# Attention values on half the rows: four full products and two 64-row pairs in place of three wide products

## The chip, the core and the metric

One NeuronCore of a Trainium2 chip runs the whole program. Its engines are TensorE (PE, with its weight loads shown as PEld), VectorE (DVE), ScalarE (ACT), GpSimd (POOL) and SyncE (SP), which here issues every DMA. The metric is the device time of one execution in microseconds, as the median of several runs.

## The reference

A macaron block on 4 sequences of 256 tokens with 512 features, all in fp32: half a feed-forward, attention, and the same half feed-forward again, each behind a layer norm and added to `x`.

```
x = x + 0.5 * ffn(layernorm(x))      # dense 512x512 + top-2 of 8 LoRA experts
x = x + attn(layernorm(x)) 
x = x + 0.5 * ffn(layernorm(x))

q, k, v = x @ wq, x @ wk, x @ wv     # 32 query heads, 8 key heads, 128 wide
q, k = rope(q), rope(k)
allowed = (j <= i) & (j > i - 128)   # a window of 128 keys
attn = softmax(where(allowed, q @ k.T / sqrt(128), min))
out = (attn @ v) @ wo
```

The change touches `attn @ v`.

## The kernel before

The work is cut into 2 halves of two sequences each, 8 key heads per half (`groups`, 16 pairs of half `h` and key head `g`), and 2 sequences per half: `units`, 32 triples (h, g, b). One unit handles 4 query heads (G) and the 256 queries of one sequence. Query, key, value and output projections use seven products of half size in place of eight (a Strassen-Winograd scheme), with sums of weights and tokens made on POOL and DVE.

**Scores** (`scores`, L730). The queries of a unit lie in 8 blocks of 32, with the four heads side by side, so that one matmul has 4 x 32 query rows. Blocks 0 to 3 (the first 128 queries) see keys up to their own block. Blocks 4 to 7 see the 128 keys of their window, and these are folded onto 128 places: the place of a key in the second half of the sequence is that of the key 128 earlier, whose turn in the window is over. `exponentials` (ACT), `normalize` (POOL) follow.

**Turning** (`turn_blocks`, L785, and `fetch`, L796). The probabilities have queries on the partitions; the value product needs keys there. DVE transposes 32x32 blocks in place (L791), one DMA for each half of the key blocks writes them to DRAM (`kept`, L792), and four DMAs, one for each of the four key blocks (L799), read them back into `turned`: partition = key place, then head, query block, query. The places that no query of a block sees are zeros set once at the start.

**Mask and values.** In the second 128 queries each place holds an old key for some queries and a new one for others. `split` (L804) writes `part`, the share of `turned` that belongs to new keys; on POOL (`affine_select`, L807) for b = 0 and for the last group, on DVE (a product with the constant `new`, L812) for b = 1. `difference` (L817) turns the second tile of values of each sequence into its difference to the first tile, and `values` (L822) then makes

```python
        for i, parts in enumerate((p0, p1)):
            po = (score_bank, mm_bank)[i](f"o{'ab'[i]}_{h}_{g}_{b}")
            for n, part in enumerate(parts):
                nc.tensor.matmul(
                    po, v[:, 2 * b + n, cols], part, start=(n == 0), stop=(n == len(parts) - 1)
                )
            nc.scalar.copy(oT[:, :, ts(i, P)], po.rearrange("p (j q) -> p j q", j=G))
```

that is, three products of 128 rows by 512 columns: `oa` = v0 with the first four query blocks, `ob` = v0 with the last four, plus (v1 - v0) with `part`. ACT copies both banks to `oT` (L832). `outputs` (L835) lets POOL make sums of `oT` and PE multiply with the output weights (`y`, L852).

**Order.** PE, DVE, ACT and POOL run in the order that the program writes; SP's DMAs are ordered by a scheduler that goes by their dependences. The loop over units looks one unit ahead. For b = 0, a string of letters sets the order: the digits are the products of the next group's queries (`queries`, `q` at L575, followed by the rotary sums on DVE, L523 and L525, and POOL, `qT` at L531), `T` and `U` turn the probabilities of the current unit, `t` is the mask, `S` the next unit's scores, `y` an output product of the unit before. For b = 1, the next key or value projection (`k` at L632, `v` at L684) stands between. In both, `values` is followed by the first products of the next keys, values or queries, and then by the first `y` product.

**Homes.** `turned` and `probs` exist once; `part` is a pool tile with one buffer. The layer norm's scaled tiles `xc` have three buffers of their own; `hl` and `ht` (router and expert columns) have homes sized for four tiles.

Of the kernel before, what the change touches and what calls it, by code (L numbers as in the profile page):

```python
# [38 lines left out]
def macaron_kernel(  # L39
# [154 lines left out]

    def by_heads(dst, make):
        make(dst, 0)
        other = sb.tile(list(dst.shape), F32, tag="by_heads", bufs=1, name=f"{dst.name}_hi")
        for j in range(1, G):
            make(other, j * BLK)
            nc.gpsimd.tensor_copy(dst[ts(j, BLK), :], other[ts(j, BLK), :])  # L200
# [32 lines left out]
    turned = const.tile([P, G, 2 * NB, BLK], F32, name="turned")  # L233
    for e in range(NB - 1):
        nc.gpsimd.memset(probs[:, e + 1 :, e, :], 0.0)
    for c in range(1, NB):
        nc.gpsimd.memset(turned[ts(c, BLK), :, :c, :], 0.0)


    old = const.tile([P, NB, BLK], F32, name="old")  # L240
    nc.gpsimd.memset(old, 1.0)
    nc.gpsimd.affine_select(
        out=old, in_=old, compare_op=ALU.is_gt,
        fill=0.0, base=0, pattern=[[-BLK, NB], [-1, BLK]], channel_multiplier=1,
    )
    new = const.tile([P, NB, BLK], F32, name="new")
    nc.gpsimd.tensor_scalar(new, old, -1.0, 1.0, ALU.mult, ALU.add)

    rank = const.tile([P, E], F32, name="rank")
    for e in range(E):  # L250
# [18 lines left out]
    def scale(t, tag):  # L269
        if (tag, t) not in moments:  # L270
            measure(t, tag)
        mv, std = moments[tag, t]
        std = std or deviation(t, tag, mv)
        rstd = sb.tile([P, 1], F32, tag="rstd", bufs=4, name=f"rs_{tag}_{t}")
        nc.vector.reciprocal(rstd, std)
        xc = sb.tile([P, D], F32, tag="xc", bufs=3, name=f"xc_{tag}_{t}")
        if tag == "f1":
            shift = sb.tile([P, 1], F32, tag="shift", bufs=4, name=f"sh_{tag}_{t}")
            nc.vector.scalar_tensor_tensor(shift, mv[:, 0:1], -1.0, rstd, ALU.mult, ALU.mult)
            cols = slice(D // 2 if t < 2 else 0, D)  # L280
            if t < 2:
                lo = slice(0, D // 2)
                nc.vector.tensor_scalar(xc[:, lo], xt[t][:, lo], mv[:, 0:1], rstd, ALU.subtract, ALU.mult)
            nc.scalar.activation(xc[:, cols], xt[t][:, cols], AF.Identity, bias=shift, scale=rstd)
        else:
            nc.vector.tensor_scalar(xc, xt[t], mv[:, 0:1], rstd, ALU.subtract, ALU.mult)
        if far(t, tag):
            nc.vector.transpose(xc, xc)
            away = dram.tile([KC, P, P], F32, tag="away", name=f"away_{tag}_{t}")
            nc.sync.dma_start(  # L290
                out=away.rearrange("c p x -> p c x"), in_=xc.rearrange("p (c x) -> p c x", c=KC)
            )
            xc = away
        moments[tag, t] = xc

    def far(t, tag):
        return tag == ("a" if t >= TPH else "f2")
# [56 lines left out]
    def ffn(tiles, tag, then):  # L354
# [22 lines left out]
        def narrow(i):  # L377
            t = tiles[i]
            if i == 0:
                state["hl"] = sb.tile([P, TPH, E * R + E], F32, tag="hl", name=f"hl_{tag}_{t0}")[:, :n, :]  # L380
            pa = score_bank(f"pa_{tag}_{t}")
            for c in range(KC):
                nc.tensor.matmul(  # L383
                    pa[:, : E * R + E], x_of(i, c), ar_sb[:, c, :],
                    start=(c == 0), stop=(c == KC - 1),
                )
            nc.scalar.copy(state["hl"][:, i, :], pa[:, : E * R + E])
# [84 lines left out]
        def gated():  # L472
            hl = state["hl"]
            pt = ps.tile([P, n, P], F32, tag="s", bufs=4, name=f"ph_{tag}_{t0}")
            for i in range(n):
                nc.tensor.transpose(pt[:, i, :], hl[:, i, : E * R], ident)
            state["ht"] = sb.tile([P, TPH, P], F32, tag="ht", bufs=1, name=f"ht_{tag}_{t0}")
            nc.scalar.copy(state["ht"][:, :n, :], pt)

        def leave(i):  # L480
            bank, t = po.pop(i), tiles[i]
# [184 lines left out]
    def project_values(h, g):  # L666
# [36 lines left out]
        def others():  # L703
            product(2, c11)
            product(4, c21)
            add(v21, c21, u2)
            product(3, c12)
            nc.scalar.copy(v11, c11)
            add(v12, c12, u2)
            difference(h, g)  # L710

        return first, both, second, others

# [71 lines left out]
    def turn_blocks(pr, name, c):  # L785

        if c == 0:
            kept[name] = dram.tile([P, NB, 2 * NB * BLK], F32, tag="kept", name=f"kept_{name}")
        if True:
            w = pr[:, c : c + 2].rearrange("p c n k -> p (c n k)")  # L790
            nc.vector.transpose(w, w)  # L791
            nc.sync.dma_start(  # L792
                out=kept[name][:, c : c + 2, :], in_=pr[:, c : c + 2].rearrange("p c n k -> p c (n k)")
            )

    def fetch(name):  # L796
        heads = kept.pop(name).rearrange("(j k) c x -> k j c x", j=G)
        for c in range(NB):
            nc.sync.dma_start(  # L799
                out=turned[ts(c, BLK), :, c:, :].rearrange("p j n q -> p j (n q)"),  # L800
                in_=heads[:, :, c, c * BLK :],
            )

    def split(h, g, b):  # L804
        part = sb.tile([P, G, NB, BLK], F32, tag="part", bufs=1, name=f"part_{h}_{g}_{b}")
        if b == 0 or (h, g) == groups[-1]:
            nc.gpsimd.affine_select(  # L807
                out=part, in_=turned[:, :, NB:, :], compare_op=ALU.is_ge, fill=0.0, base=0,
                pattern=[[0, G], [BLK, NB], [1, BLK]], channel_multiplier=-1,
            )  # L810
        else:
            nc.vector.tensor_tensor(  # L812
                part, turned[:, :, NB:, :], new.unsqueeze(1).to_broadcast([P, G, NB, BLK]), ALU.mult
            )
        return [turned[:, :, :NB, :]], [turned[:, :, NB:, :], part]

    def difference(h, g, tiles=slice(None)):  # L817

        pairs = vS[h, g].rearrange("p (b i) f -> p b i f", i=2)[:, tiles]
        nc.vector.tensor_tensor(pairs[:, :, 1], pairs[:, :, 1], pairs[:, :, 0], ALU.subtract)  # L820

    def values(h, g, b, p0, p1):  # L822
        oT = sb.tile([HD, G, S], F32, tag="oT", bufs=4, name=f"oT_{h}_{g}_{b}")
        v = vS[h, g - g % 2]
        cols = ts(g % 2, HD)
        for i, parts in enumerate((p0, p1)):
            po = (score_bank, mm_bank)[i](f"o{'ab'[i]}_{h}_{g}_{b}")
            for n, part in enumerate(parts):
                nc.tensor.matmul(  # L829
                    po, v[:, 2 * b + n, cols], part, start=(n == 0), stop=(n == len(parts) - 1)  # L830
                )
            nc.scalar.copy(oT[:, :, ts(i, P)], po.rearrange("p (j q) -> p j q", j=G))  # L832
        return oT

    def outputs(h, g, b, oT):  # L835
# [162 lines left out]
    def run(queue, n):  # L998
        for _ in range(min(n, len(queue))):
            queue.popleft()()  # L1000
# [24 lines left out]
    for u, (h, g, b) in enumerate(units):  # L1025
# [11 lines left out]
        def turn_half(c):  # L1037
            once(f"t{c}{ahead[-1]}", lambda: turn_blocks(ahead[0], ahead[-1], c))
# [9 lines left out]
        fill(left, 0)  # L1048
        if left == 1:
            nc.scalar.activation(root, eps, AF.Sqrt)  # L1050
        parts = []

        def look_ahead(at=u + 1):
            nonlocal ahead
# [4 lines left out]
            add_sums(h - 1, BPH - 1, nc.gpsimd, slice(-2, None))  # L1059
            sum_weights("v", *groups[n])  # L1060

        def part(at=(h, g, b)):
            parts.extend(split(*at))

        if b == 0 and n < len(groups):

            order = {0: "1n6kTvD2U75tS4r3n", 4: "1Eyn6TaW2U7cyXx5dtSy4re3yVn"}[len(late)]
            steps = queries(*groups[n], nc.scalar.copy, ends)  # L1070
            steps |= {
                "y": lambda: run(late, 1), "r": invert, "n": level, "S": look_ahead,
                "E": lambda: exponentials(*ahead, which=range(NB, 2 * NB)),
                "D": lambda: difference(0, 0, slice(1)),
                "W": lambda: sum_o_weights(h, g, ("t3", "t1")), "X": lambda: sum_o_weights(h, g, ("t2",)),
                "x": between_halves if (h, g) == groups[NKV + 1] else None,
                "V": lambda: sum_o_weights(h, g, ("t4",)), "v": lambda: project_v(0, 0, 2),
                "k": lambda: sum_weights("k", *groups[2]), "a": lambda: fill(left, 1),
                "T": lambda: turn_half(0), "U": turn, "t": part, "c": None, "d": None, "e": None,
            }  # L1080

            if g == NKV - 2 and h + 1 < NHALF:
                more_tokens = sum_tokens(h + 1, *(nc.gpsimd, nc.vector) * 2)
                steps |= {"c": more_tokens[3], "d": more_tokens[1], "e": more_tokens[2]}
            for step in order:
                if steps[step]:
# [2 lines left out]
        elif b == 1 and n + 1 < len(groups):  # L1089
# [24 lines left out]
            elif n % 2 == 0 and n + 2 < len(groups):  # L1114
                load_v(*groups[n + 2])
            run(late, len(late) - 1)
            for t in shifted:
                norm_attn(t, scaled=True)
        else:
# [15 lines left out]
            load_q(*groups[n + 1])  # L1135
        if b == 0 and 1 < n < len(groups):
            load_o(*groups[n])
        if not parts:
            part()
        fill(left, 2)  # L1140
        run(late, len(late) - 1)
        early = ahead[-1] == "{}_{}_{}".format(*units[u + 1]) if left > 1 else False
# [7 lines left out]
        if u == 0:  # L1150
            project_v(0, 0, 3)
            load_v(*groups[2])
        oT = values(h, g, b, *parts)
        if u == 0:
            difference(0, 0, slice(1, 2))
        if b == 0 and n + 1 < len(groups):

# [79 lines left out]
```

## Time and profile before

| | |
|---|---|
| Median of 3 runs | 740.49 us (740.28 to 740.81) |
| Profiled execution | 740.92 us, its span 739.2 us |
| PE busy | 728.7 us (99%) |
| DVE, POOL, ACT busy | 562.5, 562.1, 195.1 us |
| Granted TensorE clock | 1.0 (mean of the execution) |
| DMA | 82.87 MB on the program's queue, 35.4% of 16 engines' span |

The span runs from the first to the last instruction that the profile shows; the execution is 1.72 us longer. Busy time counts records, and matmul records overlap, since each is shown until its result is written. Idle time of an engine that is not the last to finish costs nothing.

### The profile page before, as it was taken

Reading aid. Unit: us, or ns where it says so; the run is one execution under the profiler, and the core shown is the slowest. Engines: PE = TensorE matmul, PEld = TensorE weight load, DVE = VectorE, ACT = ScalarE, POOL = GpSimd, SP = SyncE. Lnnn points to the kernel's source line nnn. Section 1 sums busy time; section 2 is a strip of 40 time slices with the busy share of each in tenths; the row PEclk is TensorE's granted clock in tenths of the full one; section 3 lists DMA queues with packets and bytes.
Section 4 is the critical chain, followed back from the end, with each engine's and each line's share of the span. In section 5 each row is a group of like instructions: output and inputs, shape, how many; then the busy total and the mean of one; then the engine's idle time right before and its main releaser. Section 6 shows DMA issues by size and latency. Waiting matters only on the chain.

```text
span 739.2 us, 11048 instructions
## 1 busy us (share of the span) xinstructions
PE 728.7 (99%) x3606; PEld 603.3 (82%) x3606; DVE 562.5 (76%) x1297; ACT 195.1 (26%) x724; POOL 562.1 (76%) x613
## 2 busy tenths in 40 slices
PE   8999999999999999998999999999999999999998
PEld 6878888888888888886888888888888888888766
DVE  5797895878786878778677867586877867795877
ACT  5520223332222212130222233222123031222331
POOL 6878878777968686859878699868686878976753
PEclk9999999999999999999999999999999999999999
DMA  9301251424245433625142424242332415433201
GB/s 315 141 1 37 89 177 44 155 65 152 92 155 137 149 98 107 186 69 187 53 167 70 137 83 152 81 166 80 118 129 68 150 53 177 116 124 84 71 29 58
DMA packets 78249, 83.58 MB, mean 113 GB/s; under 512 B 21232, under 2 KB 50928, under 8 KB 78192
## 3 DMA queue, kind: packets, MB, share of 16 engines
q1 hardware_dynamic: 78192, 82.87, 35.4%
q8 instruction: 29, 0.48, 0.3%
q14 instruction: 28, 0.23, 0.1%
HBM read 61.88 MB, written 20.97 MB: 112 GB/s over the span
## 4 chain that ended last, share of the span: by engine, by line
PE 84%; POOL 6%; DVE 5%; issue 3%; DMA 1%; SPq 0%; ACT 0%; DVEq 0%; POOLq 0%
PE q L575 24%; PE y L852 22%; PE ob L829 7%; PE v L684 6%; PE k L632 6%; PE sb L753 4%; PE sa L739 3%; PE oa L829 3%; PE p_f L419 3%; PE po_f L419 2%; PE po_f L482 1%; PE y L894 1%; POOL x L393 1%; PE pa_f L383 1%; PE pv L720 1%
## 5 line engine op out<-in xcount | busy, mean ns | idle before, releaser
L531 POOL TENSOR_TENSOR qT<-ra_q,rb_q 128x512 f32<-128x512 f32 x64 | 81.8, 1279 | 74.8 <-DVE rb_q L525 74.8
L525 DVE TENSOR_TENSOR rb_q<-q,sin_sb 64x512 f32<-64x512 f32 x128 | 88.1, 688 | 1.7
L772 ACT ACTIVATE probs<-probs,mx 128x32 f32<-128x32 f32 (+3 forms) x128 | 44.7, 351 | 144.8 <-DVE mx L742 144.8
L779 POOL TENSOR_TENSOR probs<-probs,sm 128x512 f32<-128x512 f32 x64 | 65.7, 1046 | 6.1 <-DVE sm L1031 6.1
L869 DVE TENSOR_TENSOR x<-y,x 128x256 f32<-128x256 f32 (+1 forms) x62 | 34.2, 551 | 41.5 <-PE y L852 41.3
L852 PE MATMUL y<-wot,oT 128*128 128x256 f32 x248 | 63.7, 379 | 0.4 <-DVE rb_q L525 0.4
L852 PE MATMUL y<-wo,oT 128*128 128x256 f32 x248 | 63.7, 379 | 0.0
L832 ACT COPY oT<-oa 128x512 f32<-128x512 f32 x32 | 18.7, 585 | 169.1 <-PE oa L829 169.1
L852 PE MATMUL y<-wo,oTs 128*128 128x256 f32 x244 | 62.6, 379 | 0.0
L575 PE MATMUL q<-xs,wq 128*128 128x256 f32 x256 | 60.6, 379 | 0.2 <-DVE rb_k L525 0.2
L575 PE MATMUL q<-xs,wqs 128*128 128x256 f32 x256 | 60.6, 380 | 0.0
L575 PE MATMUL q<-xa,wq 128*128 128x256 f32 x256 | 60.5, 379 | 0.0
L575 PEld LDWEIGHTS q<-xa,wq 128*128 128x128 f32 x256 | 48.5, 190 | 12.5 <-issue 4.1
L575 PEld LDWEIGHTS q<-xs,wqs 128*128 128x128 f32 x256 | 48.5, 190 | 7.3 <-PE y L852 0.4
L575 PEld LDWEIGHTS q<-xs,wq 128*128 128x128 f32 x256 | 48.5, 190 | 7.0 <-issue 0.5
L791 DVE STREAM_TRANSPOSE probs<-probs 128x512 f32<-128x512 f32 x64 | 43.7, 700 | 10.8 <-POOL probs L779 10.4
L852 PEld LDWEIGHTS y<-wo,oTs 128*128 128x128 f32 x244 | 46.4, 190 | 6.3
L852 PEld LDWEIGHTS y<-wot,oT 128*128 128x128 f32 x248 | 45.8, 190 | 6.5 <-POOL wot L171 0.8
L852 PEld LDWEIGHTS y<-wo,oT 128*128 128x128 f32 x248 | 45.9, 190 | 5.3
L523 DVE TENSOR_TENSOR ra_q<-q,cos_sb 128x512 f32<-128x512 f32 x64 | 43.9, 686 | 6.3 <-PE q L575 2.0
L772 ACT ACTIVATE probs<-sb,mx 128x128 f32<-128x128 f32 x128 | 44.6, 357 | 0.0
L126 POOL TENSOR_TENSOR oTs<-oT 128x256 f32<-128x256 f32 x31 | 22.9, 740 | 23.5 <-ACT oT L832 23.5
(220 smaller groups left out, 1726.7 us busy)
## 6 DMA issues: line engine op xcount, KB each, us to landing
wq<-in_wq_dram SPq DMA_DIRECT2D x16, 1024.0 KB, 5.6
wo<-in_wo_dram SPq DMA_DIRECT2D x16, 1024.0 KB, 5.2
kept<-probs SPq DMA_DIRECT2D x64, 256.0 KB, 2.2
wk<-in_wk_dram SPq DMA_DIRECT2D x8, 512.0 KB, 4.3
wv<-in_wv_dram SPq DMA_DIRECT2D x8, 512.0 KB, 4.1
turned<-kept SPq DMA_DIRECT2D x32, 128.0 KB, 2.6
turned<-kept SPq DMA_DIRECT2D x32, 112.0 KB, 2.9
turned<-kept SPq DMA_DIRECT2D x32, 96.0 KB, 2.6
```

What stands on the lines that cost most here:

```text
L419: nc.tensor.matmul(bank[:, ts(i, D // 2)], lhs[j][m - 1][:, c, :], weights["bs"][m - 1][:, c, :], start=(m in (1, 5, 2, 4) and c == 0), st ...
L523: nc.vector.tensor_tensor(twice(a), twice(src), angle(cos_sb), ALU.mult)
L525: nc.vector.tensor_tensor(twice(b[o : o + half, :]), twice(src[i : i + half, :]), angle(sin_sb[o : o + half, :]), ALU.mult,)
L531: nc.gpsimd.tensor_tensor(dst, view(a), view(b), ALU.add)
L575: nc.tensor.matmul(bank[:, ts(j, S)], w[:, c, ts(j, HD)], x[:, c], start=(new and j == 0 and c == 0), stop=(c == 1), skip_group_check=True,)
L632: nc.tensor.matmul(dst, w[n - 1][:, c, :], x[n - 1][:, c], start=(start and c == 0), stop=(c == 1), skip_group_check=True,)
L684: nc.tensor.matmul(bank[:, i, :], x[n - 1][:, c, i, :], w[n - 1][:, c, :], start=(start and i == 0 and c == 0), stop=(c == 1), skip_group_ ...
L772: nc.scalar.activation(dst, src, AF.Exp, bias=mx[:, n : n + 1], scale=scale, accum_out=sm[:, n : n + 1])
L779: nc.gpsimd.tensor_tensor(w, w, sm.unsqueeze(1).unsqueeze(3).to_broadcast([P, 2, 2 * NB, BLK]), ALU.mult)
L791: nc.vector.transpose(w, w)
L829: nc.tensor.matmul(po, v[:, 2 * b + n, cols], part, start=(n == 0), stop=(n == len(parts) - 1))
L852: nc.tensor.matmul(py[:, ts(i, D // 2)], lhs[n - 1][:, c, :], weights["os", h, g][n - 1][:, c, :], start=(i == 0 and c == 0), stop=(c == 1 ...
```

## The change

`values` now makes eight products. Query blocks 2 and 3 use v0 over all 128 places (128 columns each). Blocks 6 and 7 use `w`, which holds v1 in its lower 64 rows and v0 in its upper 64; blocks 4 and 5 use v0 (256 columns each). Block 0 needs only places 0 to 63, and block 1 too: block 0 runs over the lower 64 rows, and block 1 over the upper 64, for which its keys (`aside`) and values (`vD`) are kept a second time there. In blocks 4 and 5 only the lower places hold new keys beside old ones, in 6 and 7 only the upper: `part` now holds these halves, and its two products have 64 rows each. `mixture` copies the values into `vW` and `vD` on ACT; `difference` comes later in the program. The blocks are written to DRAM by four DMAs and read back by one for `turned`, one for `aside` and two for `part`, which `split` masks in place. ACT copies the two banks out in four pieces.

With it go new homes for `xc` (`ra`, `rb`, `u2`), `hl` and `ht`; three of four token sums at the half's end go to POOL, and in the order string of these units `e` comes before `S`.

```diff
-    for c in range(1, NB):
-        nc.gpsimd.memset(turned[ts(c, BLK), :, :c, :], 0.0)
...
+    part = const.tile([P, G, NB // 2, BLK], F32, name="part")
+    aside = const.tile([P, G, BLK], F32, name="aside")
...
-        xc = sb.tile([P, D], F32, tag="xc", bufs=3, name=f"xc_{tag}_{t}")
+        home, bufs = (("xc", "u2"), 1) if far(t, tag) else (("ra", "rb"), 2)
+        xc = sb.tile([P, D], F32, tag=home[t % 2], bufs=bufs, name=f"xc_{tag}_{t}")
...
-            difference(h, g)
+            mixture(h, g)
...
-            kept[name] = dram.tile([P, NB, 2 * NB * BLK], F32, tag="kept", name=f"kept_{name}")
-        if True:
-            w = pr[:, c : c + 2].rearrange("p c n k -> p (c n k)")
-            nc.vector.transpose(w, w)
-            nc.sync.dma_start(
-                out=kept[name][:, c : c + 2, :], in_=pr[:, c : c + 2].rearrange("p c n k -> p c (n k)")
-            )
+            kept[name] = dram.tile([G, NB, BLK, 2 * NB * BLK], F32, tag="kept", name=f"kept_{name}")
+        w = pr[:, c : c + 2].rearrange("p c n k -> p (c n k)")
+        nc.vector.transpose(w, w)
+        for i in (c, c + 1):
+            nc.sync.dma_start(out=kept[name][:, i], in_=pr[:, i].rearrange("p n k -> p (n k)"))
...
+        heads = kept.pop(name).rearrange("j c k x -> (c k) j x")
+        nc.sync.dma_start(out=turned.rearrange("p j n q -> p j (n q)"), in_=heads)
+        nc.sync.dma_start(out=aside[high], in_=heads[low, :, BLK : 2 * BLK])
+        for rows, n in ((low, NB), (high, NB + 2)):
+            nc.sync.dma_start(
+                out=part[rows].rearrange("p j n q -> p j (n q)"),
+                in_=heads[rows, :, n * BLK : (n + 2) * BLK],
+            )
...
+        engine = nc.gpsimd if b == 0 or (h, g) == groups[-1] else nc.vector
+        engine.tensor_tensor(part, part, new.unsqueeze(1).to_broadcast([P, G, NB // 2, BLK]), ALU.mult)
...
+        for i, rows in ((1, low), (0, high)):
+            nc.scalar.copy(vW[h, g][rows, tiles], pairs[rows, :, i])
+        nc.scalar.copy(vD[h, g][high, tiles], pairs[low, :, 0])
...
+        add(pb[:, n : 2 * n], v0, turned[:, :, 3, :], start=True, stop=True)
+        add(pa[:, n : 2 * n], v0, turned[:, :, 2, :], start=True, stop=True)
+        add(pb[:, 2 * n :], w, turned[:, :, 6:8, :])
+        add(pa[:, 2 * n :], v0, turned[:, :, 4:6, :])
+        add(pa[:, :n], v0[low], turned[low, :, 0, :], stop=True)
+        add(pb[:, :n], v0_low, aside[high], stop=True)
+        add(pa[:, 2 * n :], dv[low], part[low], stop=True)
+        add(pb[:, 2 * n :], dv[high], part[high], stop=True)
+        blocks_of = oT.rearrange("p j (n q) -> p n j q", q=BLK)
+        for i, po in enumerate((pa, pb)):
+            nc.scalar.copy(blocks_of[:, i:NB:2], po[:, : 2 * n].rearrange("p (n j q) -> p n j q", n=2, j=G))
+        for i, po in enumerate((pa, pb)):
+            nc.scalar.copy(
+                oT[:, :, P + i * S // 4 :][:, :, : S // 4], po[:, 2 * n :].rearrange("p (j q) -> p j q", j=G)
+            )
...
-            order = {0: "1n6kTvD2U75tS4r3n", 4: "1Eyn6TaW2U7cyXx5dtSy4re3yVn"}[len(late)]
+            order = {0: "1n6kTvD2U75tS4r3n", 4: "1Eyn6TaW2U7cyXx5dteSy4r3yVn"}[len(late)]
...
-                more_tokens = sum_tokens(h + 1, *(nc.gpsimd, nc.vector) * 2)
+                more_tokens = sum_tokens(h + 1, *(nc.gpsimd,) * 3, nc.vector)
...
+            if n % 2 == 0:
+                difference(*groups[n])
```

In it `n` is 128 (G x BLK), `low` and `high` are rows 0 to 63 and 64 to 127, `pa` and `pb` are two PSUM banks.

## The prediction

> **What bounds the kernel now.** I read the page's busy times first, then its chain of waits, then the matmul groups with shapes kept apart, then the chain in order of time, then the timeline of one unit.
>
> ```profile
> span 739.2 us, 11048 instructions
> PE 728.7 (99%) x3606; PEld 603.3 (82%) x3606; DVE 562.5 (76%) x1297; ACT 195.1 (26%) x724; POOL 562.1 (76%) x613
> ...
> PE 84%; POOL 6%; DVE 5%; issue 3%; DMA 1%; SPq 0%; ACT 0%; DVEq 0%; POOLq 0%
> ```
>
> TensorE is idle for 739.2 - 728.7 = 10.5 us of the span, and the chain that ended last is 84% PE. So time taken from PE's stream comes off the end nearly one for one, and time taken from DVE, ACT or POOL comes off nowhere. The profiled execution took 740.92 us, 1.72 over its span and 0.43 over the median of 740.49; I sum against 740.92 and take the 0.43 off at the end.
>
> The groups of matmuls (mean is a record's duration; a program's fp32 matmul is two records, two weight loads):
>
> ```profile
> L829 PE MATMUL ob<-part,v 128*128 128x512 f32 x64 | 33.0, 597 | 1.3 <-POOL part L807 1.0 <-DVE part L812 0.3
> ...
> L829 PE MATMUL oa<-turned,v 128*128 128x512 f32 x64 | 32.8, 593 | 0.5 <-issue 0.5
> L829 PE MATMUL ob<-turned,v 128*128 128x512 f32 x64 | 32.7, 592 | 0.0
> ...
> L684 PE MATMUL v<-wv,xs 128*128 128x128 f32 x112 | 14.8, 275 | 0.0
> ```
>
> Every group is 128*128: no matmul of before works on 64 rows, which is what the change adds. Durations overlap; the price is the spacing, from the chain in order of time (start, length):
>
> ```profile
> 216.51 1.72 PE ob L829 x4
> 218.23 1.78 PE v L684 x16
> 220.88 4.46 PE v L684 x40
> 225.35 3.46 PE y L852 x16
> ```
>
> Four 512-column records take 1.72, so a 512-column matmul costs 0.86 us. Sixteen 128-column records take 1.78: 0.223 per matmul. Sixteen 256-column records take 3.46: 0.432 per matmul. The three products of a unit are 3 x 0.86 = 2.59 us; 32 units make 82.8 us.
>
> The timeline of one b = 1 unit, for what the values wait for:
>
> ```profile
> 263.19 0.94 SPq L792 DMA_DIRECT2D kept<-probs  x2
> ...
> 265.28 2.08 SPq L799 DMA_DIRECT2D turned<-kept  x4
> ...
> 267.96 1.05 PE L739 MATMUL sa<-kT,qT 128*128 128x32 f32 x8
> ...
> 268.86 1.25 PE L753 MATMUL sb<-kT,qT 128*128 128x160 f32 x8
> ...
> 270.54 1.65 DVE L812 TENSOR_TENSOR part<-turned,new 128x512 f32<-128x512 f32 x1 [0.15 <-DMA turned<-kept]
> ...
> 271.67 1.02 PE L829 MATMUL oa<-turned,v 128*128 128x512 f32 x2
> ```
>
> The mask starts 0.15 us after the last load, PE 1.1 us after that: the transfers are close behind the end.
>
> **The products, full part.** Four full products replace part of the work: two of 128 columns and two of 256, 2 x 0.223 + 2 x 0.432 = 1.31 us.
>
> **The products, pairs.** Four matmuls over 64 rows remain: 128 low (`turned`), 128 high (`aside`), 256 low and 256 high (`part`), in this order. One after another they cost the same 1.31 us; the unit is then 2.62, 0.03 more than now, +1.1 us over 32 units. If each pair ran wholly side by side, 0.655 is saved: 1.965, -0.62 a unit, -19.9 us. These are the two ends for the overlap. I take neither. The records of one matmul sit on the same rows, so they follow each other, and PE takes records in order; then only neighbours on different halves overlap: second record of the low 128 with the first high (0.111), the next two (0.111), and second low 256 with first high 256 (0.216). That is 0.438 saved, if weights can be loaded into both halves at once. If loads follow each other, the floor shows in `sa`: eight records of 32 to 128 columns take 268.86 - 267.96 = 0.90, 0.112 each, though narrow ones need less. Loads in line then leave only about 0.23 saved. I take 0.438, since the loads belong to different rows: 2.62 - 0.438 = 2.18, -0.40 a unit.
>
> **The change of shape.** Each unit goes once from 128 rows to 64 and once back. No row shows that. Bounds: nothing (a gain is excluded, there is nothing to overlap that is not counted above), and at most a record's tail plus an uncovered weight load. The tail is duration less spacing, 0.379 - 0.216 = 0.163; the load before a matmul is 0.21 (its load row starts at 254.82 in the same view, its matmul at 255.03). So 0 to 0.37 a switch, two a unit: 0 to 23.9 us. I take half a tail, 0.08, nearer to the low end since loads of before run ahead of their matmuls everywhere: +0.16 a unit.
>
> The Trainium skill (TensorEngine Tiling (Array Packing), Key Properties) says that a change of the tiling mode drains the TensorE, which speaks against this change; it gives no time, and no run here shows it. With the whole tail of 0.163 a switch, my sum would gain 0.08 a unit instead of 0.24, 2.5 us in all.
>
> So PE gains 0.40 - 0.16 = 0.24 us a unit, 7.7 us.
>
> **Transfers.** SP issues eight a unit in place of six: four `kept` writes, one `turned`, one `aside`, two `part`. Two `kept` issues take 0.94 now; four go out by about 264.4, and the last lands 2.2 later (the page's median for `kept`), 266.6. The single `turned` load needs all four; it is 512 KB of 128x4x256, the shape of the `wk` and `wv` loads, which land in 4.3 and 4.1: 270.8. The `part` loads, issued 0.4 apart behind it on the same queue, land near 271.2; the mask (128x256; 606 ns in the row of `v` at L820, where the wider one has a median of 822) ends near 271.8. PE first needs `turned` at 271.67 and `part` some 1.6 later: margins of 0.9 and 1.4. Behind the mask DVE has the next scores' maxima, held some 0.6 us; ACT alone reads them next, and it sits idle 144.8 us for them already. In b = 0 units the mask is POOL's and today ends 5.5 us ahead of its product (290.53 against 296.07 in the next unit); behind it wait the `qT` sums, for which POOL idles 74.8 us. The price is 0 if the margins hold, and if each of 14 b = 1 units lost 0.5 us, 7 us. I take 0.5 in all.
>
> The skill (DMA: Bandwidth & Descriptors, Specifications) wants pieces of at least 512 B for line rate; the `part` and `aside` pieces are 256 and 128 B. The `xa` loads of before have 128 B pieces and land in 2.4 us, like others of their size, so here the row speaks for no extra cost.
>
> **Other engines.** `oT` comes out in four copies of 256 columns (372 ns, the L641 row) in place of two of 585. The last three follow the last matmul, so `oT` is whole some 1.1 us after it, not 0.6; the first reader, the y product, has its weights loaded 1.35 after (259.12 against 257.77). Cover gone, each unit would lose the difference. `mixture` adds three ACT copies of 64x512 a pair of groups, some 14 us in all on an engine 26% busy, hidden by its waits for `mx`. `difference` goes later on DVE, behind these copies; POOL's mask keeps its 0.73 us, DVE's halves: off the path. The renamed homes of `xc`, `hl` and `ht`, the startup tables, and one token sum that goes from DVE to POOL: nothing, hidden under PE's stream; uncovered, 1.3 us for the sum, once.
>
> **Sum.** 740.92 - 7.7 + 0.5 - 0.43 = 733.3 us.
>
> **Rivals.** *Nothing runs side by side.* Then 64 rows cost as much as 128, +1.1 us plus 0.5 for transfers: 742.1. For it: no row shows overlap. Against it: each member of a pair has its own rows and its own bank (`pa`, `pb`). The change then doesn't do what it says. *The switch eats the gain.* This one ends slower. It sits at the first 64-row matmul and at the first full one after it. It decides from 0.20 us a switch (half of 0.40); at 0.37 it costs 0.74 - 0.40 = +0.34 a unit, +10.9: about 751.9. With loads in line, 0.10 a switch is enough. For it: the tail and the load are real in the rows; against it: loads run ahead now. *The load comes late.* The overlap pays its 7.7, but `turned` misses its margin by 0.5 in the b = 1 units: +7, 739.8; no difference that counts. *No switch cost, weights in parallel*: -12.9 + 0.5, 728.1.
>
> **How the numbers follow.** 0.2%, about what a measurement of this kernel tells from no change, is 1.5 us. The overlap paying (728 to 739): 0.59, in it 0.15 for the free switch. No difference, mostly the late load or a switch near 0.20: 0.11. Slower: 0.30, of which no overlap 0.12 and the switch 0.18. Faster and slower both hold weight, so the likeliest case's own range is 728 to 739; eight in ten needs the other sides: 727 to 747, which leaves out the dearest switch and whole pairs side by side.
>
> **What would show it.** Right: in the groups, 64-row matmuls at L838; in the timeline, the eight products of a unit from first start to the next matmul in 2.3 to 2.4 us, the high 128 starting before the low one's second record ends; PE still 99% busy. A gap of 0.2 or more ahead of the first 64-row record or behind the last is the switch. A unit of 2.62 is no overlap. If PE waits at its first product for `turned`, the transfers decide. I am wrong if PE's idle time grows by more than 5 us.

## The result, and the profile after

The changed kernel takes 875.0 us (872.4 to 876.7, 4 runs) against 740.4 for the kernel before on the same chip: a ratio of 1.181, with an interval of 1.178 to 1.185. It is 134.6 us slower, far outside the range. The profiled execution took 876.0 us. Lines from its page (here and below, rows that the argument does not need are left out):

```profile
span 874.3 us, 11949 instructions
PE 767.3 (88%) x3926; PEld 641.6 (73%) x3926; DVE 553.3 (63%) x1296; ACT 215.0 (25%) x815; POOL 556.4 (64%) x612
PEclk9999889999898999899998999898999999999899
PE 45%; DMA 31%; DVE 12%; POOL 6%; issue 3%; SPq 3%; ACT 0%; DVEq 0%; POOLq 0%; ACTq 0%
```

TensorE was idle for 10.5 us of the span before; now it is idle for 874.3 - 767.3 = 107.0. Its busy time grew too, 728.7 to 767.3, although it has less to multiply. And DMA, 1% of the chain that ended last, is now 31%. The row of slices gives a reason for the second: the granted clock dips all along the execution (mean 0.941, before 1.0).

The waits (engine and what it waited for: us in total, times, longest):

```profile
POOL part L810 <- DMA part<-kept: 96.6, 16, 12.4
PE ob L838 <- DMA turned<-kept: 93.9, 26, 7.1
DVE part L810 <- DMA part<-kept: 92.1, 15, 7.3
```

PE waits at the first value product of 26 of the 32 units, for the load of `turned`. The timeline of one b = 1 unit, to set beside the one of before (SPq rows are issues: start, time that SP took, how many):

```profile
301.56 2.33 SPq L796 DMA_DIRECT2D kept<-probs  x4
304.00 0.60 SPq L100 DMA_DIRECT2D wk<-in_wk_dram  x1
306.90 0.63 SPq L801 DMA_DIRECT2D aside<-kept  x1
310.63 0.37 SPq L800 DMA_DIRECT2D turned<-kept  x1
314.90 0.77 PE L838 MATMUL ob<-turned,v 128*128 128x128 f32 x2 [4.69 <-DMA turned<-kept]
315.26 0.43 DVE L810 TENSOR_TENSOR part<-part,new 128x256 f32<-128x256 f32 x1 [6.50 <-DMA part<-kept]
```

The four writes are issued by 303.89. The load of `turned` needs all of them and goes out at 310.63, 6.7 us later. Before, the second write was issued by 264.13; the first load, which reads only the first write's blocks, went out 1.15 us after that (265.28), and the third load, the first to read the second write's, 2.45 us after it (266.58). PE now waits 4.69 us, and then the unit's products need 3.95 us from first start to the next matmul. Over these 3.95 us (314.90 to 318.85) the mean granted clock is 0.57.

A unit that does not wait looks like this (start, from first to last end):

```profile
680.42 0.38 PE L838 MATMUL ob<-turned,v 128*128 128x128 f32 x2
680.64 0.39 PE L838 MATMUL oa<-turned,v 128*128 128x128 f32 x2
680.86 0.60 PE L838 MATMUL ob<-turned,vw 128*128 128x256 f32 x2
681.29 0.90 PE L838 MATMUL oa<-turned,v 128*128 128x256 f32 x3
681.82 0.18 PEld L838 LDWEIGHTS oa<-turned,v 64*128 64x128 f32 x1 [0.33 <-issue]
682.14 0.38 PE L838 MATMUL oa<-part,v 64*128 64x256 f32 x1
682.15 0.38 PE L838 MATMUL ob<-part,v 64*128 64x256 f32 x1
682.67 1.13 PE L636 MATMUL k<-xa,wk 128*128 128x256 f32 x4
```

682.67 - 680.42 = 2.25 us (2.26 with the trace's third decimal). In the kernel before, the unit that starts at 271.67 ends with this row's start:

```profile
274.25 1.89 PE L575 MATMUL q<-xa,wq 128*128 128x256 f32 x8
```

274.25 - 271.67 = 2.58. After, the low and high products over `part` start together. The products do what the change says. It is their operands that come too late.

### The profile page after: what moved, and what is told of

The parts are those of the page before. It is cut to its first block, busy times and chain, and to the rows that moved or that the text cites. A ratio compares the mean times of both kernels' runs of the same rounds, so it can differ in the third digit from the quotient of the medians.

```text
span 874.3 us, 11949 instructions
## 1 busy us (share of the span) xinstructions
PE 767.3 (88%) x3926; PEld 641.6 (73%) x3926; DVE 553.3 (63%) x1296; ACT 215.0 (25%) x815; POOL 556.4 (64%) x612
## 4 chain that ended last, share of the span: by engine, by line
PE 45%; DMA 31%; DVE 12%; POOL 6%; issue 3%; SPq 3%; ACT 0%; DVEq 0%; POOLq 0%; ACTq 0%
DMA kept<-probs 20%; PE q L579 15%; DMA turned<-kept 10%; PE oa L838 7%; PE y L874 7%; PE ob L838 4%; PE v L688 4%; PE k L636 3%; DVE rb_q L529 2%; SPq L796 2%; DVE q L558 2%; DVE probs L794 1%; DVE ra_q L527 1%; POOL oTs L126 1%; PE p_f L423 1%
## 5 line engine op out<-in xcount | busy, mean ns | idle before, releaser
L838 PE MATMUL ob<-turned,v 128*128 128x128 f32 x64 | 18.9, 388 | 94.0 <-DMA turned<-kept 93.9
L838 PEld LDWEIGHTS ob<-turned,v 128*128 128x128 f32 x64 | 12.8, 244 | 104.5 <-issue 104.3
L850 ACT COPY oT<-oa 128x256 f32<-128x256 f32 x32 | 11.9, 372 | 311.5 <-PE ob L838 311.5
L810 POOL TENSOR_TENSOR part<-part,new 128x256 f32<-128x256 f32 x17 | 12.3, 726 | 96.6 <-DMA part<-kept 96.6
L579 PE MATMUL q<-xa,wq 128*128 128x256 f32 x256 | 65.3, 399 | 0.0
L810 DVE TENSOR_TENSOR part<-part,new 128x256 f32<-128x256 f32 x15 | 6.4, 425 | 92.1 <-DMA part<-kept 92.1
L838 PE MATMUL oa<-turned,v 128*128 128x128 f32 (+2 forms) x192 | 62.6, 431 | 0.0
L838 PEld LDWEIGHTS oa<-turned,v 128*128 128x128 f32 (+1 forms) x192 | 43.7, 261 | 20.4 <-issue 16.7
```

Source lines behind the costliest of these rows:

```text
L579: nc.tensor.matmul(bank[:, ts(j, S)], w[:, c, ts(j, HD)], x[:, c], start=(new and j == 0 and c == 0), stop=(c == 1), skip_group_check=True,)
L810: engine.tensor_tensor(part, part, new.unsqueeze(1).to_broadcast([P, G, NB // 2, BLK]), ALU.mult)
L838: nc.tensor.matmul(dst, v, p, start=start, stop=stop, skip_group_check=True)
```

## The experiments

The questions were: is the loss the products or the transfers; if transfers, which part; and what do the products give when nothing waits. All medians stand beside 740.4 to 741.3 for the kernel before on the same chip. "Idle" is span less PE busy time; busy time, idle time and clock are those of the profiled execution.

| kernel | us | ratio | PE busy | idle | clock |
|---|---|---|---|---|---|
| before | 740.4 | | 728.7 | 10.5 | 1.0 |
| after | 875.0 | 1.181 | 767.3 | 107.0 | 0.941 |
| before, after's writes | 827.1 (one run) | | 759.6 | 65.8 | 0.964 |
| after, writes by head | 868.1 | 1.172 [1.170, 1.173] | 766.6 | 99.8 | 0.945 |
| the same, other order of pairs | 869.9 | 1.173 [1.171, 1.176] | 766.4 | 97.7 | 0.944 |
| after, four loads | 850.2 (one run) | | 764.0 | 84.5 | 0.950 |
| after, writes by head and half | 817.0 | 1.103 [1.100, 1.106] | 748.9 | 71.1 | 0.967 |
| after, SP in program order | 840.2 (one run) | | 758.9 | 79.6 | 0.955 |
| after, writes by head, SP in order | 759.5 | 1.026 [1.023, 1.028] | 730.1 | 27.4 | 0.998 |
| after's products, before's transfers | 742.7 | 1.002 [1.000, 1.003] | 726.6 | 14.4 | 0.995 |
| the same without `aside` | 747.8 | 1.009 [1.007, 1.010] | 732.8 | 14.8 | 0.995 |
| the same with `aside`, tail in order | 738.9 | 0.998 [0.997, 0.999] | 725.9 | 12.1 | 0.996 |
| before's transfers, two visits to 64 rows | 754.1 | 1.017 [1.016, 1.019] | 739.9 | 13.5 | 0.992 |

**The writes alone.** The kernel before, with nothing changed but how the blocks are written:

```diff
-    kept[name] = dram.tile([P, NB, 2 * NB * BLK], ...)
+    kept[name] = dram.tile([G, NB, BLK, 2 * NB * BLK], ...)
...
-    nc.sync.dma_start(out=kept[name][:, c : c + 2, :], in_=pr[:, c : c + 2]...)
+    for i in (c, c + 1):
+        nc.sync.dma_start(out=kept[name][:, i], in_=pr[:, i].rearrange("p n k -> p (n k)"))
...
-    heads = kept.pop(name).rearrange("(j k) c x -> k j c x", j=G)
+    heads = kept.pop(name).rearrange("j c k x -> k j c x")
```

> The kernel before, with one thing of the change: the turned blocks are written by key block into the new DRAM layout (slowest dimension 4, four writes a unit in place of two); read back by four loads and multiplied as before. Theory A (writes on 4 engines): most of the loss comes back, 840 to 885, with waits of some 5 us for turned. Rivals B and C (products; reading): 740 to 746.

827.1 us: the writes alone cost 86 us, with the products of before. That is under the 840 to 885 that I had expected, but far from the 740 to 746 of the rivals. The cause can be counted. Each DMA of the kernel before leaves 16 packets of 4 bytes in the trace, which I read as one for each DMA engine that took part: 303 DMAs, 4848 such packets. This kernel has 367 DMAs and 4336 of them, 1536 short of 16 each; that is 12 for each of its 128 writes. So each write ran on 4 engines. After shows the same 367 and 4336. Its `kept[:, i]` has the shape heads x keys x columns, 4 x 32 x 256: the outermost size is 4. The Trainium skill (DMA: Bandwidth & Descriptors, Why a DMA increments its semaphore by 16 and not by 1) sets a DMA's engines by the slowest dimension of each side and "picks the largest k ≤ 16 that divides both of those dim sizes"; for 4 heads and 128 partitions that is 4, and the count agrees.

**All engines, but late.** The blocks written by head instead, four writes of 32 partitions, all behind the second transposition:

```diff
-        for i in (c, c + 1):
-            nc.sync.dma_start(out=kept[name][:, i], in_=pr[:, i]...)
+        if c == 2:
+            for j in range(G):
+                nc.sync.dma_start(out=kept[name][j].rearrange("c k x -> k c x"), in_=pr[ts(j, BLK)]...)
```

> The changed kernel, but the turned blocks are written to DRAM by head (four writes of 32 partitions, all four key blocks at once) in place of by key block (four writes whose slowest dimension is 4). Theory A, the writes: a write whose slowest dimension is 4 is carried by 4 of the 16 DMA engines, and four of them in a row land some 7 us after the last transpose, so PE waits about 5 us in a unit and comes back at half clock. Then the waits go here, PE saves what the warm units of the changed kernel show (a unit's eight products take 2.26 us against 2.59 before, 0.33 x 32 = 10.5 us), and the time is 728 to 736. Rival B, the products: 64-row matmuls, their switches and the clock are the loss; then it stays at 860 to 880. Rival C, the reading: one load for the whole block and the 128 and 256 byte pieces are late by themselves; then 780 to 860.

868.1, a miss: all 367 DMAs have their 16 packets (5872), and the time hardly moves. It falls into the range that I gave the products (860 to 880), but the trace shows another cause. The writes themselves are cured: four of 128 KB still, they land 2.2 us after their issue (the page's median), as the two of the kernel before did. So it is the engines, and not the number of the writes, that made them late. The timeline of a b = 0 unit of this kernel shows what took the place:

```profile
280.44 1.75 SPq L797 DMA_DIRECT2D kept<-probs  x4
287.95 0.39 SPq L107 DMA_DIRECT2D wq<-in_wq_dram  x1
288.52 0.38 SPq L804 DMA_DIRECT2D turned<-kept  x1
295.99 0.77 PE L842 MATMUL ob<-turned,v 128*128 128x128 f32 x2 [4.61 <-DMA turned<-kept]
```

SP's scheduler, seeing other dependences, put the 1 MB load of `wq` ahead of `turned`. SP issues it only at 287.95, 5.8 us after the last write (280.44 + 1.75 = 282.19), and PE gets `turned`, issued behind it at 288.52, only at 295.99. In most b = 1 units the cure worked: `turned` goes out about 1.9 us after the last write (310.69 against 308.76), and PE's first product at 315.25 waited 0.27 us, not 4.69. But the b = 0 units before the last two groups, all but the first at 2.3 us or less in the changed kernel, now wait over 4. With writes by head for each half, eight of 64 KB, the first four start a transposition earlier:

```diff
+        for j in range(G):
+            nc.sync.dma_start(out=kept[name][j, c : c + 2].rearrange("c k x -> k c x"), ...)
```

> The changed kernel with the writes by head (32 partitions each, so carried by all 16 engines), but for each half of the key blocks as soon as it is transposed: eight writes of 64 KB in place of four. The run by head with all four key blocks at once left the time at 868 us, but there the weight load wq (1 MB) had moved ahead of turned on the one queue; here it stays behind, though the loads wk and wv (512 KB) stay ahead in the b = 1 units. Theory A' (late transfers are the loss: few engines for the writes, and whatever stands ahead of turned on the queue): 740 to 790, waits left in b = 1 units alone. Rival B (products and their switches): 860 to 880.

817.0, 51 us less with the same bytes on all engines, and still 76 above before: a miss too, above the 740 to 790 expected. In its timeline weight loads stand ahead of `turned` as well (`wq` at 271.43, `turned` at 272.02; in the b = 1 unit `wk` at 295.50, `turned` at 296.27). I had expected `wq` to stay behind. What the order on SP is worth by itself is measured below.

**Four loads for one.** After, its writes on 4 engines kept, `turned` loaded by key block:

```diff
-        nc.sync.dma_start(out=turned.rearrange("p j n q -> p j (n q)"), in_=heads)
+        for c in range(NB):
+            nc.sync.dma_start(out=turned[ts(c, BLK)]..., in_=heads[ts(c, BLK)])
```

> The changed kernel with its four-dimension writes, but turned read back by four loads of 32 partitions in place of one load. Theory A (writes): no help, 865 to 890, PE still waits some 5 us a unit. Rival C (the one load is late): the waits shrink, below 820.

850.2, between the two ranges that I had named: with late writes, 25 us come back when a load need not wait for all four.

**SP in program order.** After, with one line changed, so that its DMAs go in the order that the program writes:

```diff
-        tc.manual_schedule(engines={Pool, Activation})
+        tc.manual_schedule(engines={Pool, Activation, SP})
```

> The changed kernel with SP's DMAs in the order of the program, the writes as they were (slowest dimension 4). Theory A' says that the four writes still land some 7 us late and PE waits: 845 to 880. If the queue's order alone were the cause: below 780.

840.2, a little under the 845 to 880 expected: order alone gives back 35. Its timeline shows the price of 4 engines bare, with nothing between the writes and the load:

```profile
289.97 2.34 SPq L796 DMA_DIRECT2D kept<-probs  x4
297.93 0.37 SPq L800 DMA_DIRECT2D turned<-kept  x1
```

The load goes out 297.93 - 292.31 = 5.6 us after the last write's issue. Both cures together, the writes by halves for b = 0 and all four blocks at once for b = 1:

```diff
+        if name[-1] == "1":
+            blocks_now = slice(0, NB) if c else slice(0, 0)
+        else:
+            blocks_now = slice(c, c + 2)
+        for j in range(G if blocks_now.stop else 0):
+            nc.sync.dma_start(out=kept[name][j, blocks_now].rearrange("c k x -> k c x"), ...)
...
+        tc.manual_schedule(engines={Pool, Activation, SP})
```

> The changed kernel with the writes by head (for b = 0 by halves, for b = 1 all key blocks at once), and SP's DMAs in the order of the program from the first layer on, so that no weight load stands ahead of turned. Theory A': nearly all waits gone, the products' 0.33 us a unit comes through: 728 to 742. Rival B (products and switches): 860 to 880. Rival C (one load and small pieces are late by themselves): 760 to 820.

759.5, above the 728 to 742 expected, and just under the 760 to 820 of the rival that the single load and its small pieces are late. Of the waits on loads this is left:

```profile
POOL part L817 <- DMA part<-kept: 40.8, 15, 9.6
DVE part L817 <- DMA part<-kept: 39.1, 14, 4.5
PE ob L845 <- DMA turned<-kept: 8.3, 11, 2.2
```

PE's wait for `turned` fell from 93.9 to 8.3; `part`, third in SP's queue, holds the masks (POOL's and DVE's waits cost only where PE needs them). So some of the loss lies with the loads, whatever the writes do: the loads of `part` are still 4% of the chain that ended last, and the next run, with the writes and loads of before, is 16.8 us faster.

**The products with the old transfers.** Writes and the four loads as before; `part` is not loaded but made from `turned`, and only `aside` keeps loads (two, 32 partitions each):

```diff
-        nc.sync.dma_start(out=turned..., in_=heads)
-        nc.sync.dma_start(out=aside[high], in_=heads[low, :, BLK : 2 * BLK])
-        for rows, n in ((low, NB), (high, NB + 2)):
-            nc.sync.dma_start(out=part[rows]..., in_=heads[rows, :, n * BLK : (n + 2) * BLK])
+        for c in range(2):
+            nc.sync.dma_start(
+                out=aside[P // 2 + c * BLK : P // 2 + (c + 1) * BLK], in_=heads[:, :, c, BLK : 2 * BLK]
+            )
...
+        for rows, n in ((low, NB), (high, NB + 2)):
+            engine.tensor_tensor(part[rows], turned[rows, :, n : n + 2], new[rows]..., ALU.mult)
```

> The changed kernel's eight products with the transfers of before: two writes a unit over all 128 partitions, four loads of 32 partitions, each for the query blocks that see its key block; part is not loaded but made in two half-row multiplications straight from turned, and only aside keeps loads of its own (two of 32 partitions). If the loss lies wholly in the transfers, PE's 0.33 us a unit (2.58 in line before, 2.25 measured in an unwaited unit after) shows in full: 740.4 - 10.5 = 730, up to 734 if the two aside loads cost SP some tenths in b = 1 units. If the 19 us that the best variant still lost against before come from the products, the ACT copies or the new homes of tiles, this kernel stays above 745.

```profile
span 741.0 us, 11961 instructions
PE 726.6 (98%) x3926; PEld 621.7 (84%) x3926; DVE 577.7 (78%) x1311; ACT 210.0 (28%) x815; POOL 572.1 (77%) x633
PE 83%; DVE 6%; POOL 5%; issue 3%; DMA 1%; ACT 0%; SPq 0%; DVEq 0%; POOLq 0%; ACTq 0%
```

742.7: 132 of the 134.6 us are gone, so the loss lay in the transfers and in the clock that fell with their waits. Set against this span, after's 133.3 us more are 92.6 of idle time (107.0 - 14.4) and 40.7 of the same products drawn out (767.3 - 726.6). Yet 730 to 734 was expected, and it stayed at 742.7. The trace shows the two main reasons. First, 24 of the 32 units take 2.26 us and four more up to 2.35, but the record after each unit is 0.10 late too (below): 0.22 us saved a unit, not 0.33. Second, the tail: at the unit at 667.5 the kernel leads by 4.1 us, at its end it is 1.8 behind.

```profile
683.22 0.46 PE L848 MATMUL oa<-turned,v 128*128 128x128 f32 x2 [1.58 <-DMA turned<-kept]
685.63 2.04 PE L426 MATMUL p_f<-wb_sb,xn_f 128*128 128x256 f32 x4 [1.94 <-DVE mx L749]
687.47 0.63 PE L848 MATMUL ob<-turned,v 128*128 128x128 f32 x2
```

In the last three units a scheduler orders PE and DVE, not the program, and it put a feed-forward product (`p_f`), which waits for DVE, behind the first value product. These units also run slowly: from 683 to 692 us the mean granted clock is 0.62.

**Without `aside`.** Blocks 0 to 3 by two full products, only the pair of `part` on 64 rows; SP issues just what it did before:

```diff
-        add(pb[:, n : 2 * n], v0, turned[:, :, 3, :], start=True, stop=True)
-        add(pa[:, n : 2 * n], v0, turned[:, :, 2, :], start=True, stop=True)
+        add(pa[:, : 2 * n], v0, turned[:, :, 0:2, :], start=True, stop=True)
+        add(pb[:, : 2 * n], v0, turned[:, :, 2:4, :], start=True, stop=True)
...
-        add(pa[:, :n], v0[low], turned[low, :, 0, :], stop=True)
-        add(pb[:, :n], v0_low, aside[high], stop=True)
```

> As the kernel with the old transfers, but without aside: blocks 0 to 3 by two full products of 256 columns, 4 and 5 with v0, 6 and 7 with w, and only the pair of part on 64 rows. SP then issues exactly the DMAs of before in their order. PE: 4 x 0.43 + 0.43 + 0.2 (pair side by side and two switches) = 2.35 a unit, 0.23 less than before: 740.4 - 7.4 = 733. Against the kernel with aside, 3 us slower if aside's loads are free, faster if they cost more than 0.1 us a unit. If something other than the transfers holds the changed kernel up, above 745.

747.8, a miss. A unit takes 2.45 us, 2.55 with the late record behind it: I had priced the switches at 0.2 a unit, and they are 0.39. At the unit at 672 it stands 0.8 us behind the kernel before; the rest is the tail again, where the scheduler put more feed-forward products in between.

**The tail put in order.**

```diff
+        with tc.manual_schedule(engines={PE}) if left < 3 else ExitStack():
             add(pb[:, n : 2 * n], v0, turned[:, :, 3, :], start=True, stop=True)
...
-            order = {..., 4: "1Eyn6TaW2U7cyXx5dteSy4r3yVn"}
+            order = {..., 4: "1Eyn6TaW2U7cyXx5dtSy4re3yVn"}
-                more_tokens = sum_tokens(h + 1, *(nc.gpsimd,) * 3, nc.vector)
+                more_tokens = sum_tokens(h + 1, *(nc.gpsimd, nc.vector) * 2)
```

> The kernel with the old transfers, with two things put back: the eight products of the last two units stay together in PE's order (in the last three units a scheduler orders PE and DVE, and put a feed-forward product behind the first of them), and the token sums at the half's end go to POOL and DVE in turn as before. If the kernel with the old transfers lost its gain in the tail (there it led by 4.1 us at the unit at 667 and ended 1.8 behind), about 5 of these come back: 737 to 738. From its trace the products give 0.32 us a unit, less 0.10 on the second record of whatever follows them: 0.22 x 32 = 7.0, so that no less than 733.7 is to be had. If the order in the tail is not the cause, it stays at 741 to 743.

738.9, 3.7 us less than without it, and with a ratio of 0.998 [0.997, 0.999] a little faster than the kernel before, by 0.2%: the lowest median here. How the order helps stays open, because the clock goes with it: without the new order, the one execution of seven with a mean clock of 1.0 took 738.6 us and the other six (0.995 to 0.998) 741.2 to 743.2; with it, eight of ten had 1.0 and took 738.6 to 739.5 (the profiled one, at 739.8, has 1.0 from 683 to 692 us). So what the tail lost may be mostly the clock. Among what lies between 738.9 and the 733.7 that the products allow are the POOL mask at the half's end (two operations, 1.85 us, begun only at 333.43; that unit takes 4.24 us) and the tail, where PE still waits 1.62 us for `turned` before the last unit but one.

**The switch.** The order of the eight products changed, so that each unit goes to 64 rows twice:

```diff
         add(pa[:, n : 2 * n], v0, turned[:, :, 2, :], start=True, stop=True)
+        add(pa[:, :n], v0[low], turned[low, :, 0, :], stop=True)
+        add(pb[:, :n], v0_low, aside[high], stop=True)
         add(pb[:, 2 * n :], w, turned[:, :, 6:8, :])
         add(pa[:, 2 * n :], v0, turned[:, :, 4:6, :])
-        add(pa[:, :n], v0[low], turned[low, :, 0, :], stop=True)
-        add(pb[:, :n], v0_low, aside[high], stop=True)
```

> The kernel with the old transfers, with the order of the eight products changed: two full ones of 128 columns, the pair of 128 columns on 64 rows, two full ones of 256, the pair of 256. So each unit goes to 64 rows and back twice, and nothing else differs. If each switch costs two lots of 0.1 us (one between the last record of one shape and the first of the other, one between the first and second records of the new shape, as the spacings in the traces look: 0.309 and 0.213 going in, 0.305 and 0.316 coming out), the two further switches add 0.38 us a unit, 12 us: 755. If a switch costs 0.08 to 0.09 once, as the prediction had it, they add 0.17 a unit, 5 to 6 us: 748.

754.1, 11.4 more than with one visit. A unit:

```profile
537.52 0.38 PE L848 MATMUL ob<-turned,v 128*128 128x128 f32 x2
537.74 0.69 PE L848 MATMUL oa<-turned,v 128*128 128x128 f32 x3
538.27 0.27 PE L848 MATMUL oa<-turned,v 64*128 64x128 f32 x1
538.48 0.70 PE L848 MATMUL ob<-turned,vw 128*128 128x256 f32 x2
539.02 0.59 PE L848 MATMUL oa<-turned,v 128*128 128x256 f32 x2
539.54 0.48 PE L848 MATMUL oa<-part,v 64*128 64x256 f32 x1
539.86 0.38 PE L848 MATMUL oa<-part,v 64*128 64x256 f32 x1
540.17 1.05 PE L691 MATMUL v<-wv,xa 128*128 128x128 f32 x7
```

From its first start at 537.52 this makes 2.65, 0.39 more for two more switches. Records of 256 columns follow each other at 0.216. After the second visit begins, 539.86 - 539.54 = 0.32: 0.10 late. Into it (539.54, where the last full record starts at 539.02 + 0.216 = 539.23) and out of it (540.17 - 539.86) it takes 0.31, each 0.09 late. So a switch costs 0.19, in two lots: one at the first record of the new shape, one at its second.

**The order inside the pairs.** The kernel with writes by head, its 64-row products in the order low, low, high, high:

```diff
         add(pa[:, :n], v0[low], turned[low, :, 0, :], stop=True)
-        add(pb[:, :n], v0_low, aside[high], stop=True)
         add(pa[:, 2 * n :], dv[low], part[low], stop=True)
+        add(pb[:, :n], v0_low, aside[high], stop=True)
         add(pb[:, 2 * n :], dv[high], part[high], stop=True)
```

> The kernel of the writes by head, with the four 64-row products in the order low 128, low 256, high 128, high 256 in place of low, high, low, high. If the halves run from queues of their own, so that order does not matter: the same time as with low, high, low, high, within 2 us. If only neighbours in program order overlap, as the prediction had it: only one 128-column record overlaps, 0.655 - 0.11 = 0.54 us a unit more, +17 us on that kernel.

869.9 against 868.1, with intervals that overlap. From its trace:

```profile
680.91 0.42 PE L842 MATMUL oa<-turned,v 64*128 64x128 f32 x1
680.93 0.42 PE L842 MATMUL ob<-aside,vd 64*128 64x128 f32 x1
681.13 0.63 PE L842 MATMUL oa<-part,v 64*128 64x256 f32 x1
```

The second record of the low 128 starts at 680.91, that of the high 128 at 680.93, ahead of the low product of 256 that stands between the two in the program. The overlap does not rest on neighbours in order.

## Why the prediction was wrong

**What bounds the kernel** was right, and it is why the miss was so dear: PE had 10.5 us of slack, so whatever held its operands was added to the end whole.

**Full products** were right: 1.31 predicted; from 680.42 to the first 64-row start at 681.82 it is 1.40, of which 0.09 is the switch.

**Pairs** were mis-sized. I had PE take records in order, so that only neighbours overlap, 0.438 saved; the halves run wholly side by side and save 0.655. **The change of shape** was mis-sized the other way: 0.08 a switch taken, 0.19 measured, 0.39 a unit for two. The errors cancel: 2.62 - 0.655 + 0.39 = 2.35, and 2.26 + 0.10 = 2.36 measured, where I had 2.34. That the unit came out near my number is luck. The switch all but reached what my rival called its deciding point (0.20), but the greater overlap paid for it. I had taken half a tail because loads run ahead of their matmuls; at the switch they do not: the weight load for the first 64-row product starts at 681.82 together with its product, 0.33 us after the load before it has ended. The Trainium skill (TensorEngine Tiling (Array Packing), Key Properties) says that a change of tiling mode drains TensorE. The 0.19 is a delay of that kind, but no run shows that it is a drain.

**Transfers** is the step that failed, by the landing of the writes: "the last lands 2.2 later (the page's median for `kept`), 266.6 ... I take 0.5 in all", 7 us at the worst. That median belongs to a write of 128 partitions x 512 columns on 16 engines. The new writes have another shape on the DRAM side and ran on 4; even with nothing in between, the load goes out only 5.6 us after the last of them is issued, where I had 2.2, and PE waited 93.9 us in 26 units, where I had 0.5 in all. I used the row for the same name and did not ask whether it had the same form; the diff shows the shape. Around that come three more faults. All of `turned` waited for the last write, which I did price, but with the wrong landing (four loads: -25 us). I assumed that SP's order would hold (`wk` and `aside` went ahead of `turned`; program order: -35 us). And I took a late load for a delay and no more. These shares are of separate runs and overlap; they don't add up.

**The clock** was in no step. In the changed kernel's trace an unwaited unit takes 2.26 us; the b = 1 units that wait about 5 us mostly take 4.41, the same instructions at about half speed (3.65 to 4.32 in others, where the clock came back on the way). The Trainium skill (TensorE: Matmul & The Clock Gate, HAM oscillation — how this bites in real kernels) warns of idle gaps over some 3.4 us. The rows agree in the main: eleven units that waited under 1.5 us took 2.26 to 2.73, one 3.11, all at a clock of 1.0. But two that waited only 1.98 and 2.29 us fell to half clock on the way and took 3.47 and 3.40, so here a shorter wait was enough, and the measurement decides. Of the 133 us, the 40.7 by which PE's busy time grew are nearly all this: weighted with the granted clock, it is 726.9 us here and 723.9 with the old transfers.

**Other engines**: nothing of what I put beside PE's stream showed while the transfers were late. The kernel with the old transfers brings out one omission: the last units, where a scheduler and not the program orders PE. There 5.9 us were lost, in part at a lower clock, which I had not looked for.

**The rivals.** *The load comes late* was the mechanism, at 739.8 and with 0.5 us a unit; it was nearly 5 us in most b = 1 units, then half the clock, and it should have been the rival that ends slower. My own test, "I am wrong if PE's idle time grows by more than 5 us", reads 96.5.

## What to carry to other kernels

Price a transfer by the row of the same shape, not of the same name: where a rewritten DMA has a small outermost size on either side, count the engines that will carry it before taking a landing time over. In a kernel where TensorE has no slack, look at what it waits for first and at the products last, because here a wait of nearly 5 us was mostly followed by some 2 us lost to the clock (4.41 us for a unit of 2.26); and where one queue serves everything and a scheduler orders it, a changed dependence can put a 1 MB load ahead of the one that matters. Half-height products that run side by side are worth their two switches only if they save more than 0.39 us a visit.

## What the runs showed of the hardware

- A DMA with an outermost size of 4 ran on 4 engines, by the count of its 4-byte packets: four such writes of 128 KB hold their reader 5.6 us after the last issue. With four writes of 128 KB on 16 engines the reader went out 1.9 us after it, and in the kernel before, with two of 256 KB, 2.45 us. SP also takes longer to issue them, 2.33 us for four against 1.75 for the writes by head.
- A change between 128 and 64 rows costs 0.19 us, half of it at the first record of the new shape and half at the second.
- Products on the two halves of the array start 3 to 7 ns apart in the changed kernel, and mostly 13 or 14 ns apart with the order low, low, high, high. The Trainium skill (TensorE: Matmul & The Clock Gate, Part 3: Packing small matmuls — row/col tiling) has matmuls start strictly in program order; in the run with the order low, low, high, high the high 128 starts ahead of the low 256, and there the measurement decides.
